# Layer 1's output projection as Strassen's seven products of 64 rows, two side by side in TensorE's columns

## The chip, the cores and the metric

One NeuronCore of a Trainium2 chip runs the whole kernel in one launch. The metric is the device time of one execution in microseconds (us), the median of several runs. Below, PE is TensorE (PEld its weight loads), DVE VectorE, ACT ScalarE, POOL GpSimd and SP the engine whose queue issues most DMAs.

## The reference, cut to what matters

A graph network of two layers on 4096 nodes with 512 features, all in float32. Layer 0 is a graph convolution; layer 1 is an attention over neighbours with positive and negative weights. Its last step, the projection by `wtrans`, is what this change is about.

```python
# layer 0
h = maximum(layernorm(x), 0)
x = x + relu((normalized_adj @ h) @ W0 + b0)
# layer 1
h = maximum(layernorm(x), 0)
e = leaky_relu(Wh1 + Wh2.T, 0.2)          # Wh1, Wh2: one number per node
attention          =  softmax(where(adj > 0,  e, -1e12), axis=1)
negative_attention = -softmax(where(adj > 0, -e, -1e12), axis=1)
h2 = concatenate([attention @ h, negative_attention @ h], axis=1)   # 4096 x 1024
x = x + elu(h2 @ wtrans)                   # wtrans: 1024 x 512
```

## The kernel before, in words

**Layer 0** takes the first half of the time. It multiplies the adjacency with the features in groups of output tiles, by Strassen's seven products for most groups (`multiply_blocks`, matmul on line 1105, 128 columns of weights and 256 moving columns), and writes the rows of `h` with their scores and masks into tables in DRAM.

**Layer 1** (`sparse_layer1`, lines 1691 to 1917) works on 64 blocks of 64 nodes, numbered `r`; blocks 2j and 2j+1 make pair j, which is also output tile j of 128 rows. Pair 16 (`PAIR0`) is worked out early, while layer 0 ends. The other 31 pairs stand in `order` (line 1856), and the loop on line 1879 takes one block in each step k, so even k is the first block of a pair and odd k the second. In step k it emits, in this order:

- `product(order[k])` (line 1799): `u` of the block. The block's 64 nodes are cut into two halves of 32. The positive and negative weights of a half are the 64 stationary columns of a matmul, and the neighbours' rows, 512 wide, move through. The two halves use the two column halves of the array, so two matmuls run side by side (line 556, `half_products`; 20 matmuls in an even step, 22 in an odd one). `cs` (line 580) is the sum for the softmax, `rl` its inverse on DVE (lines 585 and 588), and ACT's copy `us` (line 1815) divides by it.
- `gather1` (line 1739): indirect DMAs of POOL that fetch neighbours' rows for a later pair, 21 a pair in three chunks, and one DMA on SP for the pair's own rows (line 520). A chunk's buffer must have been read by the product that used it before.
- `weights(order[k + 2])` (line 1754): scores, exponentials and masks on ACT and DVE, in four PSUM banks (two `z`, two `e`), and one long reduction on DVE (line 1787).
- `turn(order[k - 1])` (line 1817): `turn_u` (line 591) transposes `us` in four PE transposes into a bank `tp`, and ACT copies it in two copies (line 602) into `uts[j]`, which holds 2 x 512 x 128 numbers: index g is the positive and negative part, then the feature chunk c, then the node.
- In odd steps from k = 3, `project1(j, 0)`, and in the even steps after it `finish1(j)`, which calls `project1(j, 1)` (line 1822). Each is four matmuls of 128 stationary columns (the tile's nodes) by 512 moving columns of `wtrans`, so one tile takes eight, and they add up in one PSUM bank. `finish1` (line 1836) then loads `x1` through SP, makes the ELU on DVE (lines 1843, 1846, 1847) and ACT (line 1844) and stores the tile through SP.

An f32 matmul leaves two matmul records in the trace: 8 of `project1` are 16 records.

PSUM is one pool of 8 banks that all of these take in turn (line 329); `bank()` hands out the next. The engines' queues follow the emitted order, apart from what the scheduler moves by its own estimate of when things are ready; instructions under `tc.keep_in_program_order` stay where they are. SBUF is laid out by hand (lines 1713 to 1729). Pools `late_mask` and `late`, on the right side, hold data of the early pair and live to the end.

The lines that set the order around the change:

```python
if k:
    turn(order[k - 1])
...
if k % 2 and k > 1:
    project1(order[k - 3] // 2, 0)
elif k > 2:
    finish1(order[k - 4] // 2)
...
finish1(order[-3] // 2)
turn(order[-1])
project1(order[-1] // 2, 0)
finish1(order[-1] // 2)
```

Of the kernel before, what the change touches and what calls it, by code (L numbers as in the profile page):

```python
# [32 lines left out]
RB = 64  # L33
SB = 32
NE = 8
# [8 lines left out]
CHUNKS = (8, 7, 7)  # L44
# [10 lines left out]
ROW = 644  # L55
# [218 lines left out]
def gcn_gat_kernel(  # L274
# [48 lines left out]
    NK = len(CAPS)  # L323
# [2 lines left out]

    sbuf = partial(tc.tile_pool, reuse_waits="tile")
    const = ctx.enter_context(sbuf(name="const", bufs=1))
    ps = ctx.enter_context(tc.tile_pool(name="ps", bufs=8, space=PSUM))
    dram = ctx.enter_context(tc.tile_pool(name="dram", bufs=1, space=DRAM))  # L330

    def bank(name):
        return ps.tile([P, 512], F32, tag="ps", name=name)

    ones = const.tile([P, P], F32, name="ones")
    nc.vector.memset(ones, 1.0)
# [253 lines left out]

    def turn_u(r, u, ut, pin=False):

        tp = ps.tile([P, FC, 2, 2, SB], F32, tag="ps", name=f"tp{r}")
        for c in range(FC):
            i = nc.tensor.transpose(  # L595
                tp[:, c].rearrange("p h g i -> p (h g i)"), u[:, c * P : (c + 1) * P], ident
            )
            if pin:
                tc.keep_in_program_order(i)
        for g in range(2):  # L600
            half = ut[:, g, :, (r % 2) * RB : (r % 2 + 1) * RB]
            nc.scalar.copy(half.rearrange("p c (h i) -> p c h i", h=2), tp[:, :, :, g, :])


    late_mask = ctx.enter_context(sbuf(name="late_mask", bufs=1, side="right"))
    late_m = late_mask.tile([P, EJ, TT * P], U8, name="late_m")
    with sbuf(name="y0", bufs=1) as y_pool, sbuf(name="wa", bufs=1) as wa_pool, sbuf(name="bits", bufs=4) as bits_pool, sbuf(name="small0", bufs=4) as small, ExitStack() as rest, ExitStack() as lists:
        list_pool = lists.enter_context(sbuf(name="list", bufs=1, side="right"))
# [101 lines left out]
        places, dealt = {}, {}  # L710

        def sum_counts(g):
            o_ps = places[g] = ps.tile([NH, NE + 1, NK + 1], F32, tag="ps", name=f"o_ps{g}")
# [781 lines left out]

        def early_pair(work, at_pool, prod, rows):

            late = ctx.enter_context(sbuf(name="late", bufs=1, side="right"))
# [192 lines left out]
    def sparse_layer1():  # L1691
        nonlocal verdict
        with ExitStack() as pools:
# [123 lines left out]
            def turn(r):  # L1817
                if r % 2 == 0:
                    uts[r // 2] = ut_pool.tile([P, 2, FC, P], F32, tag="ut", name=f"ut{r // 2}")
                turn_u(r, us.pop(r), uts[r // 2])  # L1820

            def project1(j, g):
                if g == 0:
                    halves[j] = bank(f"o1_{j}")
                for c in range(FC):
                    i = nc.tensor.matmul(  # L1826
                        halves[j],
                        uts[j][:, g, c, :],
                        wts[g][:, c, :],
                        start=g == 0 and c == 0,  # L1830
                        stop=g == 1 and c == FC - 1,
                    )
                    if c == 0:
                        tc.keep_in_program_order(i)

            def finish1(j):
                x1 = work.tile([P, F], F32, tag="x1", name=f"x1_{j}")
                nc.sync.dma_start(out=x1, in_=x1_dram[j])
                project1(j, 1)
                del uts[j]  # L1840
                po = halves.pop(j)
# [3 lines left out]
                y = work.tile([P, F], F32, tag="y", name=f"y1_{j}", bufs=1)  # L1845
                nc.vector.scalar_tensor_tensor(y, po, 0.0, x1, ALU.max, ALU.add)
                nc.vector.scalar_tensor_tensor(e, e, -1.0, y, ALU.add, ALU.add)
                nc.sync.dma_start(out=out[j * P : (j + 1) * P, :], in_=e)


            pairs = [(PAIR0 + n) % (NR // 2) for n in range(1, NR // 2)]
# [3 lines left out]
            lates, halves = {}, {}  # L1855
# [23 lines left out]
            for k, r in enumerate(order):  # L1879
                product(r)  # L1880
                if k == 0:
                    for turn_one in turns:
                        turn_one()
                    tc.keep_in_program_order(load_wt(0))
                if k % 6 == 1 and k // 6 < len(later_tables):
                    for j, n in GROUPS[-3 if k > 12 else -2 :]:
                        tc.keep_in_program_order(copy_rows(nc.sync, later_tables[k // 6], j, n))
                if k + 4 - k % 2 < len(order):
                    for a in ((0,), (1, 2))[k % 2]:
                        gather1(order[k + 4 - k % 2] // 2, a)  # L1890
                if k + 2 < len(order):
                    weights(order[k + 2])
                    if wanted and order[k + 2] % 8 == 7:
                        load_s(wanted.pop(0))
                if k:
                    turn(order[k - 1])
                if k == 1:
                    spread_s(late0, n_late, deal)
                    project1(PAIR0, 0)
                if k == 2:  # L1900
                    finish1(PAIR0)
                if k in (8, 11):
# [57 lines left out]
```

## Time and profile before

| what | value |
|---|---|
| median of 3 runs | 1995.92 us (1994.5 to 2004.08) |
| the profiled execution | 1994.23 us |
| its span, first to last instruction | 1992.4 us |
| PE busy in the span | 1876.0 us, 94% |
| projections, line 1826 | 512 matmul records, 245.2 us busy |
| `u`, line 556 | 2604 records, 596.6 us busy |
| reductions on DVE, line 1787 | 62, 3354 ns each |
| ACT copy of 128x256 out of PSUM, line 602 | 128, 385 ns each |
| layer 1 | from about 1000 us to the end |

How to read it: matmuls are pipelined, so the durations of single records overlap; two matmuls in different columns overlap wholly. What counts for PE is the distance from one start to the next, or the length of a run in the chain of waits. The chain follows the work that ended last back to what released it, instruction by instruction; "issue" in it is time in which the engine waited for nothing that the profile shows. In the groups and timelines an arrow points from what is read to what is written (`o<-wt,ut` is the projection).

### The profile page before, as it was taken

What the parts mean: (1) busy time and instruction counts of PE and PEld (TensorE: products, weight loads), DVE (VectorE), ACT (ScalarE), POOL (GpSimd) and SP (SyncE); (2) the same over time, 40 slices, a digit from 0 to 9 for tenths busy, and PEclk for the clock granted to TensorE, in tenths of its full rate; (3) what the DMA queues carried; (4) which work ended last, traced back from release to release, by engine and by line L of the source; (5) the groups of instructions that cost most, each with busy time, mean ns of one, the idle gap of its engine ahead of it and who ended that gap; (6) DMA issues with size and microseconds to landing.
All of it is one profiled execution on the core that took longest, in us unless ns stands there. A gap on an engine that the chain in (4) does not pass through costs nothing.

```text
span 1992.4 us, 24470 instructions
## 1 busy us (share of the span) xinstructions
PE 1876.0 (94%) x7692; PEld 1047.9 (53%) x7692; DVE 1274.2 (64%) x2755; ACT 937.9 (47%) x2164; POOL 822.9 (41%) x919
## 2 busy tenths in 40 slices
PE   8999999999999999999779989889898999998988
PEld 3444468888888888885343333333333333333333
DVE  6766678898889998862535655546555565554552
ACT  6777743222223222121426665556565565665651
POOL 3110000023331224213646666666666666666640
PEclk9999999999999999999979999999999999999999
DMA  9999957576948595849867788888888887877860
GB/s 374 395 330 335 337 189 236 184 230 213 294 145 264 172 288 160 271 133 314 294 229 236 251 268 293 267 306 261 287 267 294 251 263 240 276 247 246 267 197 23
DMA packets 217073, 504.31 MB, mean 253 GB/s; under 512 B 35043, under 2 KB 69123, under 8 KB 216934
## 3 DMA queue, kind: packets, MB, share of 16 engines
q0 software_dynamic: 62560, 233.71, 36.2%
q1 hardware_dynamic: 114096, 236.49, 34.7%
q10 hardware_dynamic: 40278, 32.47, 5.3%
q8 instruction: 62, 1.02, 0.2%
q14 instruction: 77, 0.63, 0.1%
HBM read 457.77 MB, written 103.45 MB: 282 GB/s over the span
## 4 chain that ended last, share of the span: by engine, by line
PE 90%; issue 5%; DMA 2%; DVE 1%; ACT 0%; another core or an unknown queue 0%; ACTq 0%; DVEq 0%; SPq 0%
PE p L1105 31%; PE u L556 30%; PE o L1826 12%; PE acc L1064 5%; PE yp L890 5%; PE q L1465 3%; PE tp L595 2%; DMA ar<-in_adj 2%; PE counts L867 1%; PE cs L1541 1%; PE tx L831 1%; PE cs L580 0%; DVE key L429 0%; DVE lst L427 0%; DMA w_sb<-in_w 0%
## 5 line engine op out<-in xcount | busy, mean ns | idle before, releaser
L506 POOL DMA_INDIRECT g<-table,idx x672 | 640.7, 953 | 419.5 <-issue 182.0
L556 PE MATMUL u<-g,p 128*64 128x512 f32 x2604 | 596.6, 597 | 40.4 <-issue 39.8
L556 PEld LDWEIGHTS u<-g,p 128*64 128x64 f32 x2604 | 185.9, 137 | 393.6 <-issue 386.9
L1765 ACT ACTIVATE z<-s,g 128x64 f32<-128x64 f32 x812 | 259.5, 320 | 52.9 <-issue 15.1
L442 POOL DMA_INDIRECT ld<-lst,off x160 | 142.9, 893 | 339.8 <-DMA ld<-lst,off 136.4
L1826 PE MATMUL o<-wt,ut 128*128 128x512 f32 x512 | 245.2, 624 | 9.6 <-issue 6.5
L1105 PE MATMUL p<-y,at 128*128 128x256 f32 x832 | 248.2, 380 | 0.6 <-issue 0.6
L1105 PE MATMUL p<-y,sums 128*128 128x256 f32 x832 | 247.4, 379 | 0.0
L1105 PE MATMUL p<-t,sums 128*128 128x256 f32 x832 | 245.5, 379 | 0.5 <-issue 0.4
L1768 DVE TENSOR_TENSOR z<-z,y 128x512 f32<-128x512 f32 (+1 forms) x124 | 80.5, 649 | 215.2 <-ACT z L1765 81.9
L1787 DVE TENSOR_REDUCE total<-p 128x128 f32<-128x1920 f32 (+1 forms) x62 | 207.9, 3354 | 2.1
L1105 PEld LDWEIGHTS p<-t,sums 128*128 128x128 f32 x832 | 158.0, 190 | 22.6 <-issue 1.2
L1105 PEld LDWEIGHTS p<-y,at 128*128 128x128 f32 x832 | 157.1, 190 | 24.2 <-issue 3.3
L1105 PEld LDWEIGHTS p<-y,sums 128*128 128x128 f32 x832 | 158.0, 190 | 21.5
L1826 PEld LDWEIGHTS o<-wt,ut 128*128 128x128 f32 x512 | 98.2, 201 | 114.7 <-issue 111.2
L1777 DVE SCALAR_TENSOR_TENSOR p<-g,z 128x512 f32<-128x512 uint8 (+1 forms) x124 | 78.4, 632 | 108.4 <-ACT z L1773 107.6
L852 ACT ACTIVATE junk<-ar 128x1024 bf16<-128x1024 f32 x128 | 134.6, 1051 | 8.1 <-DMA ar<-in_adj 4.0
L930 ACT ACTIVATE m<-at 128x1024 uint8<-128x1024 f32 x110 | 113.0, 1047 | 53.6 <-DVE prod L1020 15.3
L1777 DVE SCALAR_TENSOR_TENSOR p<-g,e 128x512 f32<-128x512 uint8 (+1 forms) x124 | 79.1, 638 | 86.2 <-DMA g<-table,idx 32.6
L1105 PE MATMUL p<-t,at 128*128 128x256 f32 x416 | 123.9, 380 | 1.2 <-DVE w L975 1.2
L1064 PE MATMUL acc<-y,at 128*128 128x512 f32 x256 | 120.2, 594 | 0.0
L890 PE MATMUL yp<-w_sb,hx_t 128*128 128x512 f32 x256 | 119.3, 610 | 0.5 <-DVE hx_t L836 0.5
(214 smaller groups left out, 1962.9 us busy)
## 6 DMA issues: line engine op xcount, KB each, us to landing
ar<-in_adj SPq DMA_DIRECT2D x128, 512.0 KB
at<-in_adj_t SPq DMA_DIRECT2D x112, 512.0 KB
table<-table SPq DMA_DIRECT2D x49, 1032.0 KB
table<-m ACTq DMA_DIRECT2D x48, 256.0 KB
g<-table,idx POOLq DMA_INDIRECT x672
g<-table SPq DMA_DIRECT2D x32, 322.0 KB
at<-in_adj_t SPq DMA_DIRECT2D x32, 256.0 KB
xr<-in_x SPq DMA_DIRECT2D x32, 256.0 KB
```

Source lines behind the costliest of these rows:

```text
L442: return nc.gpsimd.indirect_dma_start(out=lst_dram[g][e % TURNS][:, :], out_offset=bass.IndirectOffsetOnAxis(ap=off[g][:, e, c : c + 1], a ...
L506: i = nc.gpsimd.indirect_dma_start(out=gt[:, k, :], out_offset=None, in_=table[2 * n // RPT], in_offset=bass.IndirectOffsetOnAxis(ap=idx[n ...
L556: i = nc.tensor.matmul(u[h * RB : (h + 1) * RB], p[:, k, h].rearrange("p g i -> p (g i)"), row(k), start=begin and k == HALVES[r % 2][h][0 ...
L852: nc.scalar.activation(junk, ar, AF.Identity, accum_out=parts[j][:, c : c + 1])
L890: nc.tensor.matmul(yp, hx_t[j][:, c * P : (c + 1) * P], w0_sb[:, c, :], start=c == 0, stop=c == FC - 1,)
L930: nc.scalar.activation(m, at, AF.Sign)
L1064: nc.tensor.matmul(a, at[:, 0, it * P : (it + 1) * P], y0[j], start=j == 0, stop=j == NJ - 1)
L1105: i = nc.tensor.matmul(out, left[:, x * P : (x + 1) * P], right, start=jp == 0 and first, stop=jp == NP - 1 and (final or not first),)
L1765: nc.scalar.activation(z[:, c], s, AF.Identity, bias=t[:, c])
L1777: nc.vector.scalar_tensor_tensor(p[:, k : k + n, :, g], mask.rearrange(four, h=2), 0.0, x.rearrange(four, h=2), ALU.is_gt, ALU.mult,)
L1787: nc.vector.tensor_reduce(total, q, AX.X, ALU.add)
L1826: i = nc.tensor.matmul(halves[j], uts[j][:, g, c, :], wts[g][:, c, :], start=g == 0 and c == 0, stop=g == 1 and c == FC - 1,)
```

## The change

From step k = 7 on, tiles are projected by Strassen's scheme (the Winograd form), except the last. The tile's 128 x 1024 input is seen as 2 x 2 blocks of 64 nodes by 512 features (positive part, negative part), `wtrans` as 2 x 2 blocks of 512 x 256. Seven products of 64 nodes by 256 columns over 512 features take the place of eight. Two of them run side by side in the column halves of the array: they write the upper and the lower 64 partitions of one of two PSUM banks, `left` (bx) and `right` (by). The seventh is split over its features, two chunks in each column half. So a tile takes 28 matmuls of 64 stationary by 256 moving columns: 16 in part 0 (odd step), 12 in part 1 (even step).

- At k = 6 `sum_wtrans` closes PSUM's pool of eight banks and opens six banks and the two shared ones, closes the pools of the early pair, and forms the sums of `wtrans` blocks: four DVE operations of 128x1024. One overwrites the block b12 in place.
- `sum_ut`, after the turn of a pair's second block, forms the four sums of the input's blocks: four DVE operations of 128x256, two of which read the bank `tp`.
- `join_blocks1`, in `finish1`, puts the products together: four ACT copies of 64x256, three DVE additions of 64x256, one of 64x512 and one of 128x512. The ELU then reads the result in SBUF.
- In even steps from k = 6, `finish1` stands ahead of `turn` instead of behind it.
- The last tile is projected plainly by `finish_last`, first its left 256 columns and then its right ones, with the ELU and the store in halves. The overwritten block is loaded again at the second last step (`load_again`, 512 KB through SP).

```diff
-    ps = ctx.enter_context(tc.tile_pool(name="ps", bufs=8, space=PSUM))
+    new_banks("all", 8)
...
-    late_mask = ctx.enter_context(sbuf(name="late_mask", bufs=1, side="right"))
+    early = ctx.enter_context(ExitStack())
+    late_mask = early.enter_context(sbuf(name="late_mask", bufs=1, side="right"))
...
-                turn_u(r, us.pop(r), uts[r // 2])
+                tp = turn_u(r, us.pop(r), uts[r // 2])
+                if r % 2 and blocked and r != order[-1]:
+                    sum_ut(r // 2, tp)
...
+            def sum_wtrans():
+
+                new_banks("few", 6, ("left", "right"))
+                early.close()
+                pool = pools.enter_context(sbuf(name="blocks", bufs=1, side="right"))
+                blocked["t"] = t = pool.tile([P, 3, FC, H], F32, name="wt_sums")
+                blocked["s"] = pool.tile([P, 4, FC, RB], F32, name="ut_sums")
+                blocked["k"] = pool.tile([P, H], F32, name="shared")
+                b11, b12 = wts[0][:, :, :H], wts[0][:, :, H:]
+                b21, b22 = wts[1][:, :, :H], wts[1][:, :, H:]
+                op = nc.vector.tensor_tensor
+                op(t[:, 0], b22, b12, ALU.subtract)
+                op(b12, b12, b11, ALU.subtract)
+                op(t[:, 1], b22, b12, ALU.subtract)
+                op(t[:, 2], b21, t[:, 1], ALU.subtract)
...
+                b21, b22 = tp[:, :, :, 0, :], tp[:, :, :, 1, :]
+                s = [four(blocked["s"][:, n]) for n in range(4)]
+                op = nc.vector.tensor_tensor
+                op(s[2], a11, b21, ALU.subtract)
+                op(s[1], b22, s[2], ALU.subtract)
+                op(s[0], b21, a22, ALU.add)
+                op(s[3], a12, s[1], ALU.subtract)
...
+                todo = (
+                    (
+                        ((bx, top, left, a11, b11), (bx, low, left, a22, t[:, 2])),
+                        ((by, top, left, a12, b21), (by, low, left, s[:, 2], t[:, 0])),
+                    ),
+                    (
+                        ((bx, top, right, s[:, 3], b22), (bx, low, right, s[:, 0], wts[0][:, :, H:])),
+                        (
+                            (by, top, right, s[:, 1, :half], t[:, 1, :half]),
+                            (by, low, right, s[:, 1, half:], t[:, 1, half:]),
+                        ),
+                    ),
+                )[part]
+                for pair in todo:
+                    for c in range(pair[0][3].shape[1]):
+                        for out_ps, rows, cols, a, b in pair:
+                            i = nc.tensor.matmul(
+                                out_ps[rows, cols],
+                                a[:, c],
+                                b[:, c],
+                                start=part == 0 and c == 0,
+                                stop=part == 1 and c == a.shape[1] - 1,
+                            )
+                            tc.keep_in_program_order(i)
+
+            def join_blocks1(j, q):
+
+                multiply_blocks1(j, 1)
+                bx, by = blocks.pop(j)
+                k, op = blocked["k"], nc.vector.tensor_tensor
+                nc.scalar.copy(k[:RB], by[RB:, H:])
+                nc.scalar.copy(q[:RB, H:], bx[RB:, H:])
+                nc.scalar.copy(q[:RB, :H], by[:RB, :H])
+                op(k[:RB], by[:RB, H:], k[:RB], ALU.add)
+                op(k[:RB], bx[:RB, :H], k[:RB], ALU.add)
+                nc.scalar.copy(k[RB:], k[:RB])
+                op(q[:RB, H:], q[:RB, H:], k[:RB], ALU.add)
+                two = [RB, 2, H]
+                op(
+                    q[RB:].rearrange("p (a f) -> p a f", a=2),
+                    by[RB:, :H].unsqueeze(1).to_broadcast(two),
+                    k[RB:].unsqueeze(1).to_broadcast(two),
+                    ALU.add,
+                )
+                op(q, bx, q, ALU.add)
+                return q
...
-                project1(j, 1)
+                y = work.tile([P, F], F32, tag="y", name=f"y1_{j}", bufs=1)
+                if j in blocks:
+                    po = join_blocks1(j, y)
+                else:
+                    project1(j, 1)
+                    po = halves.pop(j)
...
+            def finish_last(j):
...
+                for h in range(2):
+                    cols = slice(h * H, (h + 1) * H)
+                    po = bank(f"o1_{j}_{h}")[:, :H]
+                    for g in range(2):
+                        for c in range(FC):
+                            i = nc.tensor.matmul(
+                                po,
+                                uts[j][:, g, c, :],
+                                wts[g][:, c, cols] if g or not h else b12[:, c],
+                                start=g == 0 and c == 0,
+                                stop=g == 1 and c == FC - 1,
+                            )
...
+                if k > 5 and k % 2 == 0:
+                    finish1(order[k - 4] // 2)
+                if k == 6:
+                    sum_wtrans()
                 if k:
                     turn(order[k - 1])
...
                 if k % 2 and k > 1:
-                    project1(order[k - 3] // 2, 0)
-                elif k > 2:
-                    finish1(order[k - 4] // 2)
+                    if k > 6:
+                        multiply_blocks1(order[k - 3] // 2, 0)
+                    else:
+                        project1(order[k - 3] // 2, 0)
+                elif k == 4:
+                    finish1(order[0] // 2)
+                if k + 2 == len(order):
+                    b12 = load_again()
             finish1(order[-3] // 2)
             turn(order[-1])
-            project1(order[-1] // 2, 0)
-            finish1(order[-1] // 2)
+            finish_last(order[-1] // 2)
```

More of the change, by code (lines that the diff above doesn't have):

```diff
@@ L328, in gcn_gat_kernel, with new_banks @@
     const = ctx.enter_context(sbuf(name="const", bufs=1))
-    ps = ctx.enter_context(tc.tile_pool(name="ps", bufs=8, space=PSUM))
+    psum = ctx.enter_context(ExitStack())
+    ps = {}
+    def new_banks(name, n, own=()):
+        psum.close()
+        for tag in (*own, "ps"):
+            bufs = n if tag == "ps" else 1
+            pool = tc.tile_pool(name=f"{name}{tag}", bufs=bufs, space=PSUM, reuse_waits="tile")
+            ps[tag] = psum.enter_context(pool)
+    new_banks("all", 8)
     dram = ctx.enter_context(tc.tile_pool(name="dram", bufs=1, space=DRAM))
     def bank(name):
-        return ps.tile([P, 512], F32, tag="ps", name=name)
+        return ps["ps"].tile([P, 512], F32, tag="ps", name=name)
     ones = const.tile([P, P], F32, name="ones")
@@ L591, in turn_u @@
     def turn_u(r, u, ut, pin=False):
-        tp = ps.tile([P, FC, 2, 2, SB], F32, tag="ps", name=f"tp{r}")
+        tp = ps["ps"].tile([P, FC, 2, 2, SB], F32, tag="ps", name=f"tp{r}")
         for c in range(FC):
@@ L602, in turn_u @@
             nc.scalar.copy(half.rearrange("p c (h i) -> p c h i", h=2), tp[:, :, :, g, :])
-    late_mask = ctx.enter_context(sbuf(name="late_mask", bufs=1, side="right"))
+        return tp
+    early = ctx.enter_context(ExitStack())
+    late_mask = early.enter_context(sbuf(name="late_mask", bufs=1, side="right"))
     late_m = late_mask.tile([P, EJ, TT * P], U8, name="late_m")
@@ L712, in sum_counts @@
         def sum_counts(g):
-            o_ps = places[g] = ps.tile([NH, NE + 1, NK + 1], F32, tag="ps", name=f"o_ps{g}")
+            o_ps = places[g] = ps["ps"].tile([NH, NE + 1, NK + 1], F32, tag="ps", name=f"o_ps{g}")
             for e in range(NE + 1):
@@ L1496, in early_pair @@
         def early_pair(work, at_pool, prod, rows):
-            late = ctx.enter_context(sbuf(name="late", bufs=1, side="right"))
+            late = early.enter_context(sbuf(name="late", bufs=1, side="right"))
             late_h = late.tile([P, n_late, ROW_W], F32, name="late_h")
@@ new lines, in sum_ut, with four @@
+            def sum_ut(j, tp):
+                def four(t):
+                    return t.rearrange("p c (h i) -> p c h i", h=2)
+                (a11, _), (a12, a22) = [
+                    [four(uts[j][:, g, :, x * RB : (x + 1) * RB]) for x in range(2)]
+                    for g in range(2)
+                ]
+                b21, b22 = tp[:, :, :, 0, :], tp[:, :, :, 1, :]
[5 more added lines that the diff above has]
+                op(s[3], a12, s[1], ALU.subtract)
@@ new lines, in multiply_blocks1 @@
+            def multiply_blocks1(j, part):
+                s, t = blocked["s"], blocked["t"]
+                if part == 0:
+                    blocks[j] = [
+                        ps[tag].tile([P, 512], F32, tag=tag, name=f"{tag}{j}")
+                        for tag in ("left", "right")
+                    ]
+                bx, by = blocks[j]
+                (a11, _), (a12, a22) = [
+                    [uts[j][:, g, :, x * RB : (x + 1) * RB] for x in range(2)] for g in range(2)
+                ]
+                b11, b21, b22 = wts[0][:, :, :H], wts[1][:, :, :H], wts[1][:, :, H:]
+                top, low = slice(0, RB), slice(RB, P)
+                left, right = slice(0, H), slice(H, F)
+                half = FC // 2
+                todo = (
[22 more added lines that the diff above has]
+                            tc.keep_in_program_order(i)
@@ L1838, in finish1 @@
                 nc.sync.dma_start(out=x1, in_=x1_dram[j])
-                project1(j, 1)
+                y = work.tile([P, F], F32, tag="y", name=f"y1_{j}", bufs=1)
[4 more added lines that the diff above has]
+                    po = halves.pop(j)
                 del uts[j]
-                po = halves.pop(j)
                 e = work.tile([P, F], F32, tag="eo", name=f"eo{j}", bufs=1)
@@ L1844, in finish1 @@
                 nc.scalar.activation(e, e, AF.Exp)
-                y = work.tile([P, F], F32, tag="y", name=f"y1_{j}", bufs=1)
                 nc.vector.scalar_tensor_tensor(y, po, 0.0, x1, ALU.max, ALU.add)
@@ L1848, in finish1, with load_again @@
                 nc.sync.dma_start(out=out[j * P : (j + 1) * P, :], in_=e)
+            def load_again():
+                t = g_pools[1, 0].tile([P, CHUNKS[0], ROW], I32, tag="g", name="wt_again")
+                b = t.bitcast(F32)[:, :FC, :H]
+                nc.sync.dma_start(out=b, in_=wtrans[:F, H:].rearrange("(c p) f -> p c f", p=P))
+                return b
+            def finish_last(j):
+                x1 = work.tile([P, F], F32, tag="x1", name=f"x1_{j}")
+                nc.sync.dma_start(out=x1, in_=x1_dram[j])
+                e = work.tile([P, F], F32, tag="eo", name=f"eo{j}", bufs=1)
+                y = work.tile([P, F], F32, tag="y", name=f"y1_{j}", bufs=1)
+                for h in range(2):
[10 more added lines that the diff above has]
+                            )
+                            tc.keep_in_program_order(i)
+                    eh, yh = e[:, cols], y[:, cols]
+                    nc.vector.tensor_scalar(eh, po, 0.0, None, ALU.min)
+                    nc.scalar.activation(eh, eh, AF.Exp)
+                    nc.vector.scalar_tensor_tensor(yh, po, 0.0, x1[:, cols], ALU.max, ALU.add)
+                    nc.vector.scalar_tensor_tensor(eh, eh, -1.0, yh, ALU.add, ALU.add)
+                    nc.sync.dma_start(out=out[j * P : (j + 1) * P, cols], in_=eh)
             pairs = [(PAIR0 + n) % (NR // 2) for n in range(1, NR // 2)]
@@ L1854, in sparse_layer1 @@
             with_late = (2 * pairs[0], 2 * pairs[0] + 1)
-            lates, halves = {}, {}
+            lates, halves, blocks, blocked = {}, {}, {}, {}
             order = [r for n in pairs for r in (2 * n, 2 * n + 1)]
```

## The prediction

> **What bounds the kernel now.** I read the page first, then stretches of the trace, then the chain of waits through layer 1, then one pair of row blocks in order of time.
>
> The chain on the page says TensorE nearly everywhere; the projection to be changed is its third entry:
>
> ```profile
> PE 90%; issue 5%; DMA 2%; DVE 1%; ACT 0%; another core or an unknown queue 0%; ACTq 0%; DVEq 0%; SPq 0%
> PE p L1105 31%; PE u L556 30%; PE o L1826 12%; PE acc L1064 5%; PE yp L890 5%; PE q L1465 3%; PE tp L595 2%; DMA ar<-in_adj 2%; PE counts L867 1%; PE cs L1541 1%; PE tx L831 1%; PE cs L580 0%; DVE key L429 0%; DVE lst L427 0%; DMA w_sb<-in_w 0%
> ```
>
> Busy time by stretch: layer 1 under gathers (first two rows), layer 1 after the last gather (third), then line 1105 alone in layer 0:
>
> ```profile
> 1480.00:1580.00 100.00, 90.46 (x360) 34.96 (x356) 54.30 (x67) 59.87 (x161) 65.63 (x69) 0.97 0.85 279
> 1400.00:1700.00 300.00, 274.89 (x1090) 104.84 (x1087) 161.38 (x220) 173.15 (x464) 193.38 (x205) 0.97 0.82 268
> 1930.00:1960.00 30.00, 30.00 (x125) 11.90 (x125) 13.81 (x18) 11.00 (x30) 0.00 (x0) 1.00 0.06 18
> 400.00:700.00 300.00, 298.33 (x1377) 260.47 (x1376) 1.00 0.69 220
> ```
>
> Columns: length, busy PE, weight loads, DVE, ACT, POOL, clock, DMA share, GB/s (the last row has PE and weight loads only). No engine but PE is near full. Two consecutive blocks (a pair) in the chain, start and length:
>
> ```profile
> 1347.19 3.44 PE o L1826 x8
> 1350.63 0.12 PE cs L580 x2
> 1350.74 9.59 PE u L556 x44
> 1360.33 0.59 PE tp L595 x4
> 1360.92 3.44 PE o L1826 x8
> 1364.36 0.12 PE cs L580 x2
> 1364.47 8.88 PE u L556 x38
> 1373.35 1.54 issue
> 1374.88 0.59 PE u L556
> ```
>
> A projection is two runs of 8 matmul records (an f32 matmul leaves two), 6.88 us, with no idle time in it. A pair lasts 30.4 us (1315.48, 1347.19, 1376.82 start the same half in three pairs). About 4 us of it is "issue" at the end of the even block: there TensorE starts one instruction per 0.7 to 1.4 us while gathers run, and nobody is named. After the last gather it is gone: halves start at 1929.27 and 1955.88, 26.6 us.
>
> **TensorE's own sum.** Before: 16 records of 0.43 us, 6.88 us per tile. After: 28 products of 64 output rows by 256 columns, 56 records, two at a time, so 28 steps. No row has 64 stationary columns with 256 moving ones. From one side, half of a 512-wide step is 0.215 us, and `u` runs such pairs: 44 records, 22 steps, in 9.59 us. From the other, line 1105 moves 256 columns under 128 stationary ones: 298.33 us / 1377 = 0.217 us, though each load there takes 190 ns. I take 0.215: 6.02 us.
>
> [...]
>
> ```profile
> 1308.69 1.88 PE L556 MATMUL u<-g,p 128*64 128x512 f32 x7
> 1309.12 0.14 PEld L556 LDWEIGHTS u<-g,p 128*64 128x64 f32 x2 [0.29 <-issue]
> ```
>
> Both loads of a step, 0.14 us together, lie inside the matmuls, and 0.14 is below 0.215 too. I keep 6.02: a gain of 0.86 us, on 28 of 32 tiles (calls at k = 7, 9 ... 61; the resident pair, two early tiles and the last stay plain): **-24.1 us**. It comes in the even step: part 1 is 12 steps, 2.6 us for 3.4; part 0 is 16, still 3.4.
>
> **Half-width mode.** A `u` block of 22 steps of 0.429 is 9.44 us and took 9.59: 0.15 us to enter and leave. Part 1 follows `u` in its mode; part 0 stands alone between transposes and `cs`: one more entry per tile, between 0 and 0.3 us, I take 0.15: **+4.2 us**.
>
> **The slow stretch.** I leave it at 4 us: it starts within about a us of POOL's thirteenth gather, is locked to the gathers, and the saved work lies behind it. But while instructions start one by one, those of part 1 are worth less than the `o` records that sometimes stood there: 0 to 0.4 us a pair, I take 0.1: **+3 us**. If it stretches with the instruction count (+80 on some 228 a pair), 4 becomes 5.4: +39 us, the upper end; if it shrinks, -0.5 a pair.
>
> **DVE and ACT.** Added per tile on DVE: four `sum_ut` operations of 128x256 at 0.42 (line 1093's row: 425 ns), 1.7 us; in the join three of 64x256 (at most 0.42: time goes by columns), one of 64x512 and one of 128x512 at 0.69: 2.65 us. On ACT four copies of 64x256, at most 0.385 (line 602's row): 1.5 us. DVE goes from 16.5 to 20.9 us of a pair, ACT from 18.2 to 19.7. Neither bounds by load; the question is order:
>
> ```profile
> 1284.33 0.66 PE L595 MATMUL tp<-ident,us 128*128 128x128 f32 x4
> ...
> 1286.25 3.46 DVE L1787 TENSOR_REDUCE total<-p 128x128 f32<-128x1920 f32 x1
> ...
> 1292.84 0.63 DVE L1768 TENSOR_TENSOR z<-z,y 128x448 f32<-128x448 f32 x1 [1.06 <-issue]
> ...
> 1298.56 3.60 PE L1826 MATMUL o<-wt,ut 128*128 128x512 f32 x8
> ```
>
> Let T = 1284.3 be the end of the even block's `u`. Part 0 of the next tile would start where the `o` run at 1298.56 does, less 0.87: T+13.4. It needs both shared banks (the join's last add) and the four sums. DVE is free of the reduction at T+5.4; join 2.65, ELU three x 0.69 plus 0.1 of waiting, sums 1.7, two small `rl` operations 0.3: T+12.2. Margin 1.2 us, cost **0**. The weights of the block after next move back by up to 4.4 us; they are ready at 1303.05 and used after 1314.8, so 11 us cover them. If the margin goes, everything on TensorE's queue waits behind part 0, including the next `cs` and `u`. Behind the ACT copy that waits for DVE's two adds stand exponentials and the `us` copy; that copy's transposes come a whole block later. One step of `finish1` moves ahead of `turn`: its x1 load and out store go onto SP some us apart from now (the store later by the join, T+10.7 instead of 7.4), ahead of the own-row load at T+11, whose user is some 14 us behind it. POOL is passed by nothing: 0.
>
> **Banks.** Six for seven tiles a step instead of eight for seven and a half. Each user reuses the bank of the one six places back: `u` that of a `z` read 13 us earlier, `cs` that of the previous `u`, copied out 2 us earlier. 0 us.
>
> **Once.** At k = 6 four DVE operations of 128x1024, about 1.24 each (0.42 at 256 columns and 0.69 at 512 give 0.27 per 256): 5 us beside `u`; I take 1.5 of 0 to 5: **+1.5**. At the end the last ELU halves: 0.69+0.64+0.69 become 0.42+0.39+0.42, -0.8, and the final store halves too, about -0.3; but the join's ACT copies stand before the last `ut` copies, 0 to 2.2, I take +1.1: **0**.
>
> **Sum.** -24.1 + 4.2 + 3 + 1.5 = -15.4. The profiled execution took 1994.23 us (span 1992.4 and 1.8 around it): 1979. The median of the runs is 1995.92, 1.7 above: 1980 to 1981. I say **1980**.
>
> **Rivals.**
> - *Absorbed* (chance 0.2): the gain is taken back by a new wait of 0.2 to 0.9 us a tile, at part 0 or in the slow stretch: 1986 to 2005, about 1993. For it: the margin of 1.2 us is thin, and slow dispatch is tied to gathers that do not get shorter. Against: POOL has 4 us of waits in a pair.
> - *Part 0 waits for DVE* (0.16), the one on the other side. If DVE takes both halves of the next weights (0.63 and two of 0.62, twice: 3.7 us) before join and sums end, they end at T+15.9, 2.5 us late, on each of 28 tiles: 1980 + 70 = 2050; with one half first, 0.7 us late: 2000. It decides against the change from 0.55 us a tile. For it: those operations are ready at T+8.5, before the ELU ends. Against: DVE's order today follows the program's, and join and sums are emitted first.
> - *Weight loads exposed* (0.04): 28 x (0.6 + 0.15) + 4.5 = +26, 2020. [...]
> - *Forecast* (0.6): 1968 to 1986, the low end with the 0.15s at nothing.
>
> Half a per cent, 10 us, is about what a measurement of this kernel can tell from no change. By it: faster 0.58 (below 1986), same 0.22, slower 0.2. The range, 1970 to 2008, takes in the absorbed case; beyond it lie about 0.05 below and 0.13 above.
>
> **What would show it.** Right: the two parts in the chain at 3.4 and 2.6 us, a pair of 29.7 us, `issue` still near 4 us a pair. [...] Wrong altogether if a pair stays at 30.4 us with shorter projections: then gathers, not TensorE, set it.

## The result, and the profile after

The changed kernel takes 2099.01 us (median of 6 runs, 2091.6 to 2117.75), the unchanged one beside it 1997.49 (6 runs): 1.0513 times as long, 95% interval 1.0483 to 1.0544. The forecast was 1980, the top of the range 2008. The profiled execution took 2099.37 us, with a span of 2097.6 and a mean granted clock of 0.955; before, these were 1994.23, 1992.4 and 0.980.

First the page: span, TensorE's own line, the group of `u` matmuls (line 566 now, 556 before), and the DMA queue that the page marks "instruction". Of after:

```profile
span 2097.6 us, 27278 instructions
...
PE 1942.1 (93%) x8828; PEld 1119.3 (53%) x8828; DVE 1371.8 (65%) x3014; ACT 978.1 (47%) x2277; POOL 829.9 (40%) x919
...
q8 instruction: 71, 1.16, 0.2%
...
L566 PE MATMUL u<-g,p 128*64 128x512 f32 x2604 | 691.2, 634 | 115.0 <-issue 107.6
```

Of before:

```profile
q8 instruction: 62, 1.02, 0.2%
...
L556 PE MATMUL u<-g,p 128*64 128x512 f32 x2604 | 596.6, 597 | 40.4 <-issue 39.8
```

The same 2604 `u` records, which the change doesn't touch, are busy 95 us longer and have 75 us more idle time ahead of them, nearly all of it "issue": the profile names nobody they wait for. DVE and ACT are no nearer to full than forecast. One line of DVE's is new on the page of after, and will matter below:

```profile
L595 DVE RECIPROCAL rl<-cs 128x1 f32<-128x1 f32 x64 | 10.4, 163 | 166.7 <-remote 138.4
```

Next the stretches, with the columns as in the prediction. The first two are the same windows as there, the third lies behind this kernel's last gather:

```profile
1480.00:1580.00 100.00, 88.62 (x453) 40.13 (x449) 58.35 (x87) 57.56 (x156) 58.77 (x62) 0.94 0.73 235
1400.00:1700.00 300.00, 259.37 (x1292) 114.71 (x1293) 167.75 (x250) 162.22 (x436) 172.15 (x181) 0.93 0.74 239
2030.00:2060.00 30.00, 30.00 (x172) 13.00 (x170) 18.12 (x28) 14.93 (x40) 0.00 (x0) 1.00 0.10 36
```

In 300 us under gathers TensorE was idle for 25 us before (274.89 busy) and for 41 us now, and the clock fell from 0.97 to 0.93. In the window behind the last gather it is never idle and has its full clock, as before. So the time is lost under the gathers, mostly in two parts. From 1100 us to the last gather, the gaps between matmuls add up to 66.5 us before and 112.4 after: +46. And the mean clock, over the span, cost 0.020 x 1992.4 = 40 us before and 0.045 x 2097.6 = 94 after: +54. Of these 54, 11 fall into time in which TensorE was idle anyway, so that the two together are some 89 of the 105 us between the two spans. Under those gathers the traces have the clock at half in 6 spells before (37.5 us) and in 24 after (146.8 us).

What the idle time looks like, in order of time. POOL's rows are the gathers. Before, one run of 13 gathers (the two chunks that an odd block's product frees):

```profile
1357.18 1.04 POOL L506 DMA_INDIRECT g<-table,idx  x1 [2.60 <-PE u L556]
...
1360.76 3.60 PE L1826 MATMUL o<-wt,ut 128*128 128x512 f32 x8
...
1364.40 8.95 PE L556 MATMUL u<-g,p 128*64 128x512 f32 x38
...
1372.31 0.94 POOL L506 DMA_INDIRECT g<-table,idx  x1 [0.30 <-issue]
1374.88 1.35 PE L556 MATMUL u<-g,p 128*64 128x512 f32 x2 [1.54 <-issue]
```

After, the same run:

```profile
1388.71 0.95 POOL L516 DMA_INDIRECT g<-table,idx  x1 [4.41 <-DVE y L1934]
...
1396.44 2.90 PE L566 MATMUL u<-g,p 128*64 128x512 f32 x12
...
1399.07 0.95 POOL L516 DMA_INDIRECT g<-table,idx  x1 [0.30 <-issue]
1400.13 0.59 PE L566 MATMUL u<-g,p 128*64 128x512 f32 x1 [0.79 <-issue]
...
1401.55 0.59 PE L566 MATMUL u<-g,p 128*64 128x512 f32 x1 [0.84 <-issue]
```

Before, the slow stretch begins at 1373.35, 16.2 us after the run's first gather (14.8 in the median of the runs), with the thirteenth. After, it begins at 1399.34, 10.6 us after the first gather, with the ninth. In both, one instruction starts every 0.7 us (a load and a matmul take turns), and most of those that start late wait for no semaphore (189 of 295 in the runs of 13 after). Counting starts in the trace (an instruction is a record of a matmul or a load) gives the rule: the stretch begins some 120 TensorE instructions after the run's first gather in both kernels, and ends about 3 us after its last one is issued. Only the change's part 0, 64 short instructions in 3.4 us where the plain half has 16, gets TensorE to the 120th so much sooner.

Not only TensorE's starts are late in this run; what waits for its results is late too. After:

```profile
1396.13 0.38 PE L590 MATMUL cs<-ones,total 128*128 128x1 f32 x2
...
1398.34 2.81 ACT L1777 ACTIVATE z<-s,g 128x64 f32<-128x64 f32 x8
...
1398.70 3.20 DVE L1799 TENSOR_REDUCE total<-p 128x128 f32<-128x1792 f32 x1
...
1407.18 5.85 PE L566 MATMUL u<-g,p 128*64 128x512 f32 x22 [0.29 <-issue]
1407.34 0.17 DVE L595 RECIPROCAL rl<-cs 128x1 f32<-128x1 f32 x1 [5.44 <-remote]
```

`rl`, on DVE, waits for nothing but `cs`. `cs` was done by 1396.5 and DVE had been idle since the reduction ended at 1401.9, yet `rl` starts at 1407.34, when TensorE runs freely again. ACT meanwhile goes through eight operations at 0.35 us each. After, `rl` is more than a us late in this way in 26 of 57 blocks, before in 3 of 57.

The projection itself costs nearly what was forecast. Part 0 begins thus, and `cs` follows 3.6 us after the first start:

```profile
1427.39 0.43 PE L1914 MATMUL left<-wt,ut 128*64 128x256 f32 x1
1427.40 0.43 PE L1914 MATMUL left<-wt_sums,ut 128*64 128x256 f32 x1
1427.66 0.38 PE L1914 MATMUL left<-wt,ut 128*64 128x256 f32 x1
...
1431.00 0.38 PE L590 MATMUL cs<-ones,total 128*128 128x1 f32 x2
```

The experiments ran on three chips: on that of E1 to E4 the unchanged kernel takes 1857 us at a clock of 0.996 and TensorE is not starved under gathers (E1: busy for 299.40 us of 300), on those of E5 to E8 and E9 to E12 it takes 2013 and 2000 and is, so each run is read against the unchanged kernel beside it. E1 to E4 are also single executions, so a chip and a set of runs are not told apart here.

### The profile page after: what moved, and what is told of

The parts are those of the page before. It is cut to its first block, busy times and chain, and to the rows that moved or that the text cites. A ratio compares the mean times of both kernels' runs of the same rounds, so it can differ in the third digit from the quotient of the medians.

```text
span 2097.6 us, 27278 instructions
## 1 busy us (share of the span) xinstructions
PE 1942.1 (93%) x8828; PEld 1119.3 (53%) x8828; DVE 1371.8 (65%) x3014; ACT 978.1 (47%) x2277; POOL 829.9 (40%) x919
## 5 line engine op out<-in xcount | busy, mean ns | idle before, releaser
L566 PE MATMUL u<-g,p 128*64 128x512 f32 x2604 | 691.2, 634 | 115.0 <-issue 107.6
L566 PEld LDWEIGHTS u<-g,p 128*64 128x64 f32 x2604 | 221.5, 145 | 530.5 <-issue 504.7
L1785 ACT ACTIVATE e<-z 128x512 f32<-128x512 f32 (+1 forms) x124 | 67.2, 542 | 202.2 <-DVE z L1780 181.2
L595 DVE RECIPROCAL rl<-cs 128x1 f32<-128x1 f32 x64 | 10.4, 163 | 166.7 <-remote 138.4
L812 ACT ACTIVATE rrb<-rrb 128x1 f32<-128x1 f32 x32 | 6.5, 203 | 214.5 <-DVE rrb L811 169.9
```

Of the source, the lines that this page charges most:

```text
L566: i = nc.tensor.matmul(u[h * RB : (h + 1) * RB], p[:, k, h].rearrange("p g i -> p (g i)"), row(k), start=begin and k == HALVES[r % 2][h][0 ...
```

## The experiments

Two theories. **Supply**: during a run of gathers TensorE works off some 120 instructions at full speed and then gets one every 0.7 us until the gathers have landed; the change spends them sooner. **Work**: the sums, copies and short or half-width matmuls cost the time themselves.

### E1 to E4: one execution each

E1, the unchanged kernel with each 512-column product in four of 128 columns:

```diff
+for q in range(4):
+    cols = slice(q * P, (q + 1) * P)
     i = nc.tensor.matmul(
-        halves[j], uts[j][:, g, c, :], wts[g][:, c, :], ...
+        halves[j][:, cols], uts[j][:, g, c, :], wts[g][:, c, cols], ...
```

> The kernel before, with each 512-wide projection matmul cut into four of 128 columns, all else as before: TensorE's work stays at about 6.9 us a tile, but a tile takes 128 TensorE instructions (matmuls and weight loads) instead of 32, 64 of them in the odd step, as many as part 0 of the change has. Supply theory (in both traces the slow stretch begins about 120 TensorE instructions after a run of thirteen gathers starts, and then one instruction starts per 0.7 us until the gathers have drained): the 120 are used up near 10 us instead of 14.5, the slow stretch grows from 4-5 to 8-10 us a pair, 2080 to 2140 us. Join theory (the change lost its time to the sums and the join on DVE and ACT): 1995 to 2005. Bank and order theory (six banks, finish1 ahead of turn): 1995 to 2005.

E2, the changed kernel without `sum_ut` and without the join:

```diff
-                if r % 2 and blocked and r != order[-1]:
-                    sum_ut(r // 2, tp)
...
-                k, op = blocked["k"], nc.vector.tensor_tensor
-                nc.scalar.copy(k[:RB], by[RB:, H:])
...
-                op(q, bx, q, ALU.add)
-                return q
+                return bx
```

> The changed kernel without the four sums of a tile and without the join: the products read blocks of ut in place of the sums, and the ELU reads the bank bx, so the projection's values are not those of the reference; TensorE's instructions are all there. Supply theory: about as slow as the change, 2075 to 2105 us. Join theory: what was predicted for TensorE alone, 1970 to 1985 us. Bank and order theory: about 2099.

E3 and E4, the unchanged and the changed kernel without layer 1's gathers:

```diff
                 k = pairs.index(n)
+                if k > 1:
+                    gath.setdefault(n, {})[a] = gath[pairs[k % 2]][a]
+                    return
```

> The kernel before with no gathers and no own-row loads after the second pair of the loop: the later pairs reuse the rows of the first two, so their values are wrong, the compute engines' work is the same. Supply theory: no slow stretch, pairs of 26.6 us, about 110 us less from it and some 15 from the clock: 1865 to 1890 us. Join theory and bank and order theory say nothing of this one alone; it is the partner of the next.

> The changed kernel with the same gathers left out. Supply theory: the arithmetic gain shows once nothing starves TensorE: 15 to 22 us below the partner without gathers. Join theory and bank and order theory: the loss of 100 us stays, the changed kernel is 60 to 105 us above its partner.

Measured: 1867.31, 1854.46, 1853.67 and 1848.46 us, one run each, beside 1857.14 for the unchanged kernel. There was no slow stretch to test. E1's row for the same window:

```profile
1400.00:1700.00 300.00, 299.40 (x1781) 159.84 (x1782) 189.11 (x254) 200.29 (x539) 218.38 (x231) 1.00 0.90 294
```

TensorE is full, at full clock, with 1781 matmul records in 300 us under gathers, and these gathers follow each other in runs of 21 and more; so neither the number of instructions nor the length of a run does harm by itself. E3 and E4 still give the arithmetic undisturbed. A pair lasts 26.60 us in E3 and 26.12 in E4 (medians): 0.48 a tile. Net, E4 is only 5.2 us faster than E3, where 15 to 22 were expected: -13.4 for 28 tiles, +1.8 that lie ahead of layer 1's first block, and some 6 us once, around the step that sums the weights, and at the end. The changed kernel, whole, was not run on this chip.

### E5: the changed kernel again

> The changed kernel as it is, beside the unchanged one on the chip of these four runs. The supply theory (under the row gathers TensorE is handed an instruction only every 0.70 us from about the 120th on until the gather queue drains, and the change puts 64 instructions instead of 16 into that part of a pair): where the unchanged kernel takes about 1997 us and shows the slow stretch, 2080 to 2120 us, and the stretch 10 us long a pair against 4 to 5; where the unchanged kernel takes about 1857 us and shows no slow stretch, 1850 to 1870 us. The rival (the sums on VectorE and the copies on ScalarE hold TensorE up, whatever the supply does): about 100 us slower than the unchanged kernel in either case.

2135.74 us against 2012.74: 1.059 (1.0544 to 1.0636), with the stretch from 10.3 to 18.5 us of a run of 13: slower than the 2080 to 2120 expected, beside an unchanged kernel that is slower too. Both theories stand; it is the yardstick for the next three. The first line of its chain of waits, which in the profile shown above breaks off at the last ELU:

```profile
PE 72%; issue 10%; POOL 6%; DMA 4%; DVE 3%; another core or an unknown queue 3%; ACT 2%; POOLq 0%; DVEq 0%; ACTq 0%; SPq 0%
```

"issue" was 5% before. From 1100 us to the last gather it is 17.0% of this chain, and was 8.2% before.

### E6: part 0 beside part 1, in the even step

```diff
-                if j in blocks:
+                if j in split:
+                    multiply_blocks1(j, 0)
                     po = join_blocks1(j, y)
...
-                        multiply_blocks1(order[k - 3] // 2, 0)
+                        split.add(order[k - 3] // 2)
```

> The changed kernel with the first part of the block products (32 products, 64 instructions) moved from the odd step, where the long run of gathers is issued, into the even step right ahead of the second part. All sums, copies and products stay. Supply theory: where the slow stretch exists, it shrinks from 10 us a pair to 7 or less, as 64 instructions leave it, and the time falls from 2099 to 2010 to 2050 us; where it does not exist, the time stays within 10 us of the changed kernel's. Rival (VectorE and ScalarE): all 112 instructions of a tile now stand behind the last sum, so the time does not fall, and may rise by up to 3.4 us x 28 = 95 us.

2163.97 us, 1.0738 (1.0683 to 1.0794): a miss for the supply theory as I had put it. TensorE's waits, and the stretch in order of time:

```profile
PE left L1914 <- issue: 30.9, 21, 2.4
PE right L1914 <- issue: 12.8, 9, 2.4
PE u L566 <- issue: 11.3, 12, 2.2
```

```profile
1649.19 0.38 PE L1914 MATMUL left<-wt,ut 128*64 128x256 f32 x1
1649.20 0.38 PE L1914 MATMUL left<-wt_sums,ut 128*64 128x256 f32 x1
1649.41 0.38 PE L1914 MATMUL left<-wt,ut 128*64 128x256 f32 x1
1650.83 0.38 PE L1914 MATMUL left<-wt,ut 128*64 128x256 f32 x1 [1.03 <-issue]
1653.62 0.38 PE L1914 MATMUL left<-wt_sums,ut 128*64 128x256 f32 x1 [2.42 <-issue]
...
1656.03 0.63 PE L1914 MATMUL left<-wt_sums,ut 128*64 128x256 f32 x1
1656.17 0.63 PE L1914 MATMUL left<-wt,ut 128*64 128x256 f32 x1
1656.45 0.63 PE L1914 MATMUL left<-wt_sums,ut 128*64 128x256 f32 x1
```

But the miss is not the rival's, which wants waits on VectorE or ScalarE: the waits are "issue" again. The run of 13 did what was expected: its first idle time moved from 10.3 to 13.0 us, at the 119th instruction. What I had not counted is the pair's other run, of 8 gathers. Its last gather is issued 8.8 us after its first, and whatever holds TensorE lets go at 10.7. In E5 one of 24 is starved; here all 112 short instructions of a tile fall into it, TensorE reaches the 114th after 9.6 us, and 15 of 20 such runs in the trace are starved. Four times the two runs ran together into one of 21 gathers, with 11 us idle; there the idle time began only at the 133rd to 153rd instruction, so 120 is no constant. Moving short instructions only chooses which run starves.

### E7: the plain projection wholly in the odd step

```diff
                     project1(order[k - 3] // 2, 0)
+                    if k > 6:
+                        project1(order[k - 3] // 2, 1)
+                        done.add(order[k - 3] // 2)
...
-                project1(j, 1)
+                if j not in done:
+                    project1(j, 1)
```

> The unchanged kernel with both halves of the plain projection (32 instructions of 512 columns) in the odd step, from k = 7 on. Supply theory: these are slow, few instructions, 0.43 us apiece; 16 of them more in the run of gathers mean that more time has passed, and more of the queue is drained, by the 120th instruction, so the slow stretch shrinks from 4 to 5 us a pair to about 2.75 and the time falls from 1997 to 1950 to 1970 us where the stretch exists; where it does not, within 10 us of 1857. Rival (the order of the steps does not matter to TensorE, only the amount of work): no change in either case.

1998.12 us against 2012.74: 0.9915 (0.9888 to 0.9941). The direction is the one expected, 15 us where 27 to 47 were: the first idle time moved only from 14.8 to 15.4 us of the run. It is the one kernel here that computes all and beats the unchanged one, by 0.9%, without Strassen.

### E8: E1 where the stretch exists

> The unchanged kernel with each 512-column product of the projection cut into four of 128 columns: no sums, no copies, no 64-row blocks, 64 instructions instead of 16 in each half. Supply theory: where the slow stretch exists, 48 more instructions in the odd step lengthen it to 8 to 11 us a pair, and the time rises from 1997 to 2080 to 2140 us; where it does not exist, 1860 to 1870 us, as measured once. Rival (sums and copies are the cause): 2005 to 2015 us, only the cost of the short instructions.

2178.32 us, 1.0802 (1.0756 to 1.0847): more than the 2080 to 2140 expected. No sum, no copy and no 64-row block is in it:

```profile
1400.00:1700.00 300.00, 262.37 (x1294) 137.47 (x1295) 132.82 (x171) 143.14 (x384) 160.26 (x170) 0.93 0.72 231
```

It looks like the changed kernel's row (259.37 busy, clock 0.93), with DVE at 133 instead of 168 us. The same file ran at full clock without idle time in E1. Cutting the matmuls up is enough to cause the whole loss, given the stretch.

### E9: the changed kernel without sums and join, where the stretch exists

The edit is E2's.

> The changed kernel without the four sums of ut and without the joining copies and additions (tiles multiplied as they are, the output read from one bank: part of the computation is left out), all 28 tiles' 56 products and loads kept. Supply theory: where the unchanged kernel takes 1997 to 2013 us, this one takes 2090 to 2140 us like the changed one, since TensorE's instructions are the same and VectorE's work is not what it waits for; where the unchanged kernel takes 1857 us, 1850 to 1860. Rival (the sums and copies cost it): no slower than the unchanged kernel.

2107.97 us against 1999.83: 1.0532 (1.0485 to 1.0579), as slow as the change (1.0513 and 1.059). Taking the sums and the join off DVE (141 us busy in the window for 168 in the changed kernel) frees nothing that these runs can tell. The file is that of E2, where no `rl` is late; here 26 of 58 are:

```profile
1400.00:1700.00 300.00, 265.16 (x1309) 119.25 (x1307) 140.92 (x184) 156.54 (x420) 173.45 (x182) 0.93 0.75 242
```

### E10 and E11: a run of 6 gathers instead of 13

```diff
                 k = pairs.index(n)
+                if k > 1 and a == 2:
+                    gath.setdefault(n, {})[a] = gath[pairs[k % 2]][a]
+                    return
```

> The changed kernel with the last 7 of a pair's 21 row gathers left out after the second pair (old rows are used: part of the computation is left out), so that a run of 13 gathers becomes one of 6 and the run of 8 stays. TensorE's and VectorE's work is unchanged. Supply theory: a run of 6 is drained some 9 us after its start, before TensorE has issued the 115 instructions (9.5 us) after which it starves, so the slow stretch is gone and the time falls by over 200 us to 1850 to 1880 us. Rivals (sums, short instructions or 64-column blocks cost it): the time stays over 1950 us, as their work is still there.

> The unchanged kernel with the same 7 gathers of a pair left out after the second pair (part of the computation is left out): the control to the run before it. Supply theory: 1850 to 1880 us, and the changed kernel under the same cut is 0 to 10 us faster than this one, as the arithmetic of the blocks promised. Rival: the change stays about 100 us slower.

1896.51 us for the changed kernel and 1883.65 for the unchanged one, beside 1999.83 for the unchanged kernel uncut. The cut takes 116 us from that one, and over 200 from the changed kernel, which took 2099 and 2136 whole. E10's row, then E11's:

```profile
1400.00:1700.00 300.00, 298.57 (x1708) 136.80 (x1704) 219.78 (x347) 214.69 (x581) 151.19 (x158) 1.00 0.69 217
```

```profile
1400.00:1700.00 300.00, 300.00 (x1264) 116.23 (x1262) 187.85 (x254) 204.06 (x548) 150.06 (x159) 1.00 0.71 217
```

A third fewer gathers, still back to back for 6 and 8 at a time, and the idle time, the half clock and nearly nine tenths of the change's loss are gone (12.9 us left of some 105), with all its sums, copies and short matmuls in place. Supply wins over work. Both runs came out above the 1850 to 1880 us expected, by 16 and 4 us, and the changed kernel not 0 to 10 us ahead but 13 behind. Of the 16.3 us between the two profiled spans, 4.6 lie in layer 0, which the change doesn't touch, 7.1 come once between the first and the eleventh block, 3.8 in the blocks after and 0.8 at the end: a pair gains nothing here (26.80 against 26.60 us, medians). What takes the gain is a rest of the stretch: the odd block's `u`, which falls into the run of 8, takes 10.27 us to the next transpose and not 9.59, because TensorE is slow for a moment in it: in 12 of 20 such blocks one start comes 0.6 to 0.9 us after the one before it, at the 117th to 127th instruction of the run. `rl` is late in no block of either run.

### E12: the dose between

E1's edit with two pieces of 256 columns.

> The unchanged kernel with each 512-column product of the projection cut into two of 256 columns: 32 instructions instead of 16 in each half. The dose between the unchanged kernel (16, 2013 us beside it) and the cut in four (64, 2178). Supply theory: the 120th instruction comes 16 x 0.107 = 1.7 us earlier, the stretch is as much longer, and the time is 35 to 60 us over the unchanged kernel's on a chip that shows the stretch, 0 to 5 us where it does not. Rival (only matmuls of 128 or 64 columns of weights and outputs are slow, not their number): within 10 us of the unchanged kernel.

2031.82 us against 1999.83: 1.0167 (1.0114 to 1.022), +32 us, just under what was expected (its profiled execution is the fastest of four, 2016.85 us, so the trace shows less of it). With 16, 32 and 64 instructions in a half the plain projection takes 1.000, 1.017 and 1.080 of the unchanged kernel's time.

The runs of 13 gathers, worked out from the traces (medians; idle is the mean of a run):

| kernel | first idle after | at instruction | last idle ends | idle a run |
|---|---|---|---|---|
| unchanged | 14.8 us | 121 | 18.4 us | 2.55 us |
| E7, both halves in the odd step | 15.4 | 113 | 18.6 | 2.36 |
| E12, in two | 14.0 | 125 | 18.4 | 2.67 |
| changed | 10.6 | 121 | 18.3 | 4.22 |
| E5, changed again | 10.3 | 117 | 18.5 | 5.25 |
| E9, no sums | 10.5 | 121 | 17.7 | 4.11 |
| E6, parts together | 13.0 | 119 | 18.5 | 4.42 |
| E8, in four | 9.3 | 112 | 17.7 | 4.75 |

The time of the first idle moves by 6 us, the instruction at which it comes stays between 112 and 125, and the end stays with the gathers.

"Supply" is a name, and more than the runs show. They show that the loss goes with the number of TensorE's instructions in a run of gathers. Whether instructions come in late or something that leaves TensorE is held back, such as a signal, they don't say, and the late `rl` speaks for the second. It goes by the count as well: where `cs` is some 30 to 40 instructions into a run of 13 (before, E6, E7), `rl` follows at once; where it is the 66th (E12) or the 98th (changed, E5, E8, E9), `rl` is 5 to 9 us late in the median, though at the 66th and the 98th TensorE itself still starts freely.

A rival that no run tests is the trace. In E1 the landing of a DMA leaves 16 records of its semaphore (4286 for 269 DMAs issued between 1400 and 1700 us), and E2 to E4 are as complete. In the same window the trace of before holds 28% of that number and after 34%, E5 to E9 and E12 22 to 37%, and E10 and E11, which are nearly free of the stretch, 48 and 52%. So the traces in which TensorE is starved have lost most of these records. One thing may hold back both, or the recording may be what holds TensorE back. Every time given here comes with a traced span and clock; what the kernels take without a trace is not known. It also means that releasers are missing in these traces, and "issue" or "remote" can stand for one.

## Why the prediction was wrong, point by point

- **The slow stretch** is the step that failed: "I leave it at 4 us: it starts within about a us of POOL's thirteenth gather, is locked to the gathers, and the saved work lies behind it." Only its end is locked to the gathers. Its beginning is locked, in a run of 13, to a count of instructions, and that the 121st coincided with the thirteenth gather was chance: one kernel's trace can't tell the two apart. The term, +3 or 0.1 us a pair, measured 4.5 us a pair: +109 on the 24 pairs reckoned below.
- **The bound for it**, +39, "if it stretches with the instruction count (+80 on some 228 a pair)", had the right cause and the wrong law. I scaled the stretch by the pair's count. What counts is how early the 120th instruction comes: from 14.8 to 10.6 us of a run whose gathers end at 18.4, so 3.6 us became 7.7. And I had left the clock out: nearly half of the 89 us found above is work at the half clock that goes with such a stretch (43 us). In the trace of after the steps of line 1914 are 0.427 us (median) at half clock and 0.216 elsewhere; E6's last rows above have 0.42 (1656.03 to 1656.45). The spells at half clock last 3.4, 6.8 or 10.2 us. Counted from the last start ahead of the first late one (over 0.55 us apart), all 6 before begin 2.4 to 3.1 us into a stretch and 23 of the 24 after 3.5 to 6.7 us into one; the other 20 stretches before with three late starts or more, 2.8 to 4.8 us long, have none. What sets the half clock off was not shown.
- **TensorE's own sum**, -24.1 + 4.2, or 0.71 us a tile, was right in sign and half as much again as what E3 and E4 give, 0.48. The steps are 0.21 us as forecast; going in and out of half width costs 0.38 us a tile where the sum had 0.15. In E4 part 0 takes 3.60 us to `cs` and part 1 2.69 us, and the transposes ahead of part 0 and the `cs` behind it take 0.1 us more each, of which the even block's `u` gives 0.1 back. The weight loads don't lengthen a step: in part 0 of after (1427.39 to 1428.96) each step of 0.21 us has two loads of 0.14 us that lie beside its matmuls.
- **DVE and ACT**, 0, stands (an addition of 64x256 took 0.41 us, one of 64x512 0.70): E9 shows no cost of the sums under the stretch, and without gathers a pair with the sums (E4) lasts 26.12 us, as one without them does under gathers (E2).
- **Once**, +1.5 of 0 to 5: measured 6 to 7 (E3 against E4, and again E11 against E10). **Banks**, 0: no run tests the six banks alone. The end, 0: from the last transposes on, E4 took 17.0 us and E3 16.4.
- **The rivals.** "Part 0 waits for DVE" named the right side but the wrong cause; in the 300 us window of after TensorE waited 2.3 us for `rl` and 0.8 us for `ut_sums`. For "Weight loads exposed" no run shows the 0.6 us a tile that its sum uses; the steps are 0.21 us, and that puts it out. "Absorbed" held the thought that slow dispatch eats the gain, without seeing that it could eat more than the gain.
- **The whole**, by the lengths of pairs, which take in idle time, slow starts and clock at once. Over 24 pairs, from the 13th block of the loop on, a pair lasts 30.65 us before and 34.73 after (means), and without gathers 26.63 (E3) and 26.19 (E4). So the stretch with its half clock costs 4.0 us a pair before and 8.5 after, +109 us on the 24; the arithmetic takes 11 off, which leaves +98. The twelve blocks ahead of them, with the one-off, make +14, the end -1, and what lies ahead of layer 1's first block, which the change doesn't touch, came out 6 us faster in this execution: 105 in all. Not settled: why the single executions of E1 to E4 show no stretch with the same kernel.

## What to carry to other kernels

Before cutting matmuls into more and shorter ones, look under the densest DMA bursts for starts that come one by one with "issue" as the only releaser; if they are there, the number of TensorE's instructions counts as well as its cycles, and a saving of 7% of a projection's time that costs four times the instructions in one place can lose. To find what a stretch is locked to, count instructions from the start of the burst in more than one version: an unchanged trace shows one coincidence only. And where a wait has no releaser, look at who waits for that engine, and at how many records the trace should have had.

## What the runs showed of the hardware

- Under a run of 13 row gathers, one per 1.25 us, TensorE starts about 120 instructions freely and then one per 0.7 us until some 3 us after the last gather is issued; in the runs of 21 of E6 it is 133 to 153. Runs of 6 and of 8 end first and do little harm (E10 and E11: 12.9 us left of some 105), unless 114 instructions fit into 9.6 us (E6). In such a run what waits for TensorE can be 5 to 9 us late before TensorE itself is slow (`cs` and `rl`).
- The arrival of code is not what the stretch is locked to. A packet of `q8` is 1.02 MB / 62 = 16.4 KB. That they are TensorE's code is an estimate from the counts: E1 has 1536 matmul records and 1536 loads more than before and 74 packets for 62, 256 records for each one more, and after the change there are 1136 and 1136 more and 71 packets. But these packets don't stand with the stretches. Before, they came at 1255.9, 1291.1, 1327.1 and 1363.2 us, the stretches began at 1249.4, 1280.0, 1310.6, 1340.8 and 1373.3. What holds TensorE at the 120 was not found.
- The same kernel takes 1857 us on the chip of E1 to E4 (one execution) and 1997 to 2013 elsewhere. In the traces of the first, the stretch, the half clock after it, the late `rl` and the loss of records are all missing.
